# An RWKV block on one core: the planner's cost of a transfer, and a new order for every engine

## The chip, the cores and the metric

The kernel runs on one core of a Trainium2 chip. The core has five engines with a queue of instructions each: TensorE (PE; its weight loads are listed as PEld), VectorE (DVE), ScalarE (ACT), GpSimd (POOL) and SyncE (SP). SP only issues transfers (DMAs); ACT issues some too. An engine works through its own queue in order, and waits at an instruction until what it needs from other engines or from transfers is there. The metric is the time of one execution on the device in microseconds (us), lower is better.

## The reference

One RWKV-6 block over a batch of 8 sequences of 256 tokens and 512 channels, in 32 heads of 16, all in float32. Cut to what matters:

```python
xn = ln(x, ln1); sx = token_shift(xn, state[:, 1])
xxx = tanh((xn + sx * maa_x) @ maa_w1)                  # five groups of 32
x5 = xn + sx * (maa_stack + xxx @ maa_w2)               # k, decay, v, r, g inputs
w = exp(-exp(time_decay + tanh(x5[1] @ decay_w1) @ decay_w2))
r, k, v = x5[3] @ Wr.T, x5[0] @ Wk.T, x5[2] @ Wv.T      # 32 heads of 16
g = silu(x5[4] @ Wg.T)
def step(s, (r, k, v, w)):                              # 256 steps in time
    a = k[:, :, :, None] * v[:, :, None, :]
    return a + w[..., None] * s, einsum(r, u * a + s)
att = group_norm(scan(step)) * gn_w + gn_b
x = x + (att * g) @ Wo.T
xn2 = ln(x, ln2); sx2 = token_shift(xn2, state[:, 0])
rr = sigmoid((xn2 + sx2 * ffn_maa_r) @ ffn_Wr.T)
kk = relu((xn2 + sx2 * ffn_maa_k) @ ffn_Wk.T) ** 2
x = x + rr * (kk @ ffn_Wv.T)
```

## The kernel before, in words

**Work per sequence.** Each of the 8 sequences (b) passes three stages, with channels on the 128 partitions and 256 tokens along the row, mostly as two tiles of 256 channels each (q = 0, 1).

- `inputs_of_scan`: x is loaded (`xt<-in_x`), normed and transposed on TensorE (L503); ACT scales it into `xn` (L509); POOL takes the token shift `sx` (L512); `shifted` makes the first mix (ACT L523, POOL L525); small matmuls (L568, L581, L603) and DVE and POOL (L612, L614) make the five mixed inputs; `project` (L538) multiplies them by the resident weights Wk, Wv, Wr, Wg, and ACT copies or activates the results (L648, L657).
- `scan`: the recurrence runs on VectorE's scan instruction. ACT's queue writes v to DRAM (`vo<-v`, L695). For each of 4 blocks of channels and 4 groups i, SP reads it back as a broadcast over 16 partitions into a tile `vs` (`vs<-vo`, 512 KB, 16 per sequence). ACT sets the first column of it (L711), VectorE multiplies it by k (L714) and scans it into `st` (L716), POOL multiplies `st` by r (L719), and 32 matmuls gather the four groups (L727).
- `rest`: the group norm (ACT L745, PE L753, ACT L758, DVE L760); its scale goes to the partitions that need it in 8 small row copies for each of two tiles (`sq<-sq`, `rk<-sq`, 32 KB, issued by SP) and into `att` (POOL L784, ACT L788), then times g (POOL L790). Then the projection by Wo (`project_tokens`, L553), the second norm and mixes, and the projections by ffn_Wk (L538), ffn_Wr and ffn_Wv (L553) up to the output (DVE L821, POOL L823, `out<-o`). These four weights aren't resident: each is streamed anew for every sequence in two tiles of 512 KB (`Ws<-in_wo`, `Ws<-in_fk`, `Ws<-in_fr`, `Ws<-in_fv`) through a pool of four tiles `Ws`.

All transfers but `vo` are made by the helper `dma` and issued at L359 on SP, in one queue.

**The order of the work.** Nothing is emitted as it is written. Each operation is added to a `Plan` with its engine, an estimated duration, what it writes and reads, and its emitter. There are 2482 of them. The three stages of different sequences are planned to overlap: sequence b's `scan` beside b+1's `inputs_of_scan` and b-1's `rest`. `sequence` gives every operation a rank out of the written table `TURNS` (a permutation of 0 to 2481, in 25 rows: one for the loads at the start, then one for each stage of each sequence). `order` then goes through them as a list scheduler: among the operations whose predecessors have been placed, it takes the lowest rank, puts it off if no buffer of its pool is free, and gives it a start and an end by the durations. The buffer that it takes from a pool is the last one that came free by then. At the end all are sorted by their planned start and emitted, so every engine's queue has the order in which `order` placed them. `TURNS` is the result of a search that is not part of the kernel; the planned end (`span`) is there for it to go by.

**A transfer in the plan.** The engine that issues it (called DMA in the plan) is taken for `us` = 0.6. Then the transfer goes over one `wire`, in turn with all others, at a pace in KB per us, and is there a `lag` after it left the wire. At most eight are in flight: `lanes` holds the landings of the last eight, and an issue waits for the oldest of them. The lag is `LATENCY["DMA"]` (for `vo`, which ACT issues, `LATENCY["ACT"]`) plus what the caller passes: 1.6 for `vs`, 1.2 for `vo`, 0.3 for the row copies.

Of the kernel before, what the change touches and what calls it, by code (L numbers as in the profile page):

```python
# [13 lines left out]
NB, T, E = 8, 256, 512  # L14
# [53 lines left out]
class Plan:  # L68
# [4 lines left out]
    LATENCY = {"PE": 0.3, "DVE": 0.18, "ACT": 0.16, "POOL": 0.12, "DMA": 1.1}  # L73
# [15 lines left out]
    def add(self, engine, us, outs, ins, emit, mode=None, into=(), lag=0.0, kb=0, part=False):  # L89
        outs, ins, into = ([getattr(b, "buf", b) for b in bs] for bs in (outs, ins, into))  # L90
        op = Op(engine, us, outs, ins, emit, mode)
        op.lag, op.wire = self.LATENCY[engine] + lag, kb / 290
# [18 lines left out]
    def stage(self):  # L111
# [6 lines left out]
        316 390 152 382 416 413 475 586 386 300 368 425 948 654 392 44 107 100 185 187 379 151 569 87 545 560 70 602 544  # L118
        66 557 362 54,
        128 192 383 294 166 325 399 223 324 410 351 473 231 254 329 213 338 296 364 175 207 537 19 570 524 371 332 236  # L120
        13 233 232 52 604 287 366 216 712 572 584 556 471 540 615 432 42 45 618 206 677 519 297 527 668 20 428 122 484
        724 398 58 583 673 795 414 241 895 805 75 641 41 607 887 239 752 783 784 261 642 613 47 822 859 694 651 683 855
        357 850 472 397 482 194 523 249 789 897 730 777 791 199,
        215 224 589 276 103 201 278 36 141 619 637 344 120 179 552 253 69 229 157 168 275 794 172 359 568 336 743 920
        251 350 726 839 954 508 707 775 335 643 370 485 751 934 939 219 424 806 346 825 542 129 477 870 1049 1013 901
        240 812 1142 1161 1199 593 975 1063 779 51 1050 178 450 979 421 496 910 448 936 976 1001 749 985 381 848 1002
        952 1172 914 1016 1184 117 610 1123 314 490 1186 722 538 1200 115 412 1217 907 871,
        376 339 452 530 692 408 235 820 461 468 464 669 880 506 470 924 1004 288 658 419 282 1100 995 501 1130 315 438
        1196 930 415 792 719 1211 579 829 807 348 944 330 625 974 1236 462 648 1139 1118 740 852 1084 729 823 925 1232
        1097 274 1210 312 289 427 1209 900 700 1276 867 649 1289 1227 838 1225 188 949 1322 571 1372 796 1292 148 773  # L130
        1195 337 904 1273 1293 1247 1418 1336 1203 1423 318 631 1381 270 354 286 1344 298 682 1466 1096 1467,
        422 1367 1411 1443 95 955 711 174 1262 1468 1456 14 18 457 440 499 163 1334 227 139 234 1491 200 96 1492 843
        1093 1508 1525 1082 1190 1363 1556 653 1112 1171 951 1311 183 781 1037 1044 1582 1083 1590 992 1597 1384 1185
        1310 1622 1429 459 1602 672 420 798 725 541 1117 883 1608 1108 971 1699 1514 844 1631 1688 63 1513 608 474 1640
        1667 1545 817 1397 1007 815 1349 1257 1716 946 238 1765 1669 1309 1755 1653 505 1725 1151 967 1776 1808 189 1802
        1567 1591,
        627 1628 1672 1721 86 1665 1569 1576 1568 1572 1786 577 1204 762 1073 94 293 373 349 539 290 1798 1626 978 1434
        511 1506 1831 1649 1836 40 268 1848 429 387 1401 1126 1129 659 76 1170 1867 903 1166 1313 353 1223 281 634 591
        1470 1393 1924 1436 1791 1538 507 1943 1951 941 1955 28 1882 1368 245 1883 996 1544 1875 59 343 1733 621 378
        1540 1886 588 811 776 614 1392 1661 1908 1921 790 1944 1956 265 1942 1095 1318 1913 363 1280 1998 2019 733 2006  # L140
        1668 2015,
        1079 1069 1070 1074 1072 1577 1714 980 1930 1945 1134 1124 1982 1220 1260 1268 1208 1964 1328 221 244 2012 1999
        1133 1990 1194 1879 1719 2028 1283 91 1287 2050 832 1571 1584 592 1558 1463 1548 1751 638 2044 480 1895 33 272
        1954 1237 1853 1984 1580 2099 340 15 2002 144 2117 1331 754 1644 1675 2076 2086 2129 2068 1596 2027 2107 384
        1421 1424 2065 1465 1624 2043 1893 2009 1231 1358 1937 921 2109 656 1103 2173 2177 818 2119 2146 2154 2126 1647
        10 2207 2110 1587 2196 1634 1809,
        1408 2017 403 2123 623 865 893 1286 1010 186 2150 1102 2157 1224 958 504 1920 2156 1658 1789 1018 1988 1386 1437
        2185 17 1618 1899 2190 834 2194 90 2203 786 1104 1865 1718 1856 727 1554 1619 2253 965 1757 1840 1980 1748 1766
        1962 1143 1154 1121 2267 1305 1793 147 1312 2273 2279 93 2300 761 2212 2105 2104 2216 2238 1923 2237 1315 1712
        1316 885 886 1502 2208 1021 1749 1353 1754 467 2291 1164 1145 130 1430 1756 2281 2270 1314 2101 2290 1376 2244  # L150
        2324 1632 1852 2333 1504 1503,
        1559 2161 2073 1062 133 1060 226 85 195 2274 2264 1605 1858 1614 170 1085 2285 190 196 417 670 2297 1648 628
        2054 322 2318 1623 1555 2323 1887 714 696 766 2328 24 2330 703 664 1179 2158 5 744 2340 1402 2375 2343 2277 2350
        2339 1362 957 1345 2287 380 881 280 2378 2386 1333 2414 1267 702 1738 2387 1694 1404 2363 2345 1600 1997 2360
        1168 1812 2352 2368 826 1727 2379 1565 2251 2400 2374 326 856 2412 2095 2023 1356 2390 2402 2091 2191 479 1850
        2418 299 2427 1635 2460,
        304 389 830 772 447 927 25 30 797 940 29 119 34 543 205 718 375 800 622 431 785 165 915 894 202 667 650 248 495
        735 882 220 911 301 994 258 943 919 559 809 889 701 945 660 456 916 746 458 888 260 666 1017 863 913 65 646 60
        1149 676 851 67 1024 1045 1008 1012 7 8 896 1116 879 518 121 999 1053 446 639 1127 1092 1025 771 307 878 847
        1188 747 1177 1051 699 1167 1019 1022 1132 968 736 39 11 1155 993 1076 585 587 1158 1094 1181 1065 483 1206 50,  # L160
        611 732 739 1099 1009 1265 814 465 1405 113 1255 533 55 88 449 1202 26 1214 502 171 1193 872 127 1242 214 1256
        793 1285 1087 4 1212 497 1284 681 1299 1352 1303 906 1294 16 1351 492 522 1291 478 1323 567 1046 1295 969 1339
        491 828 1234 868 1342 689 1238 1403 1106 821 1330 1327 1395 764 827 1416 763 1320 984 1382 292 1317 1326 1041
        1373 1383 1189 1350 860 1399 1427 68 1432 1481 1370 1355 1445 132 1464 922 1398 1219 1433 1444 1218 1152 1448
        970 1469 1450 1407 1252 1447 1462 273 1499 1509,
        674 1483 566 708 1440 1449 1532 1052 1642 38 1536 198 1417 1486 977 1343 1375 728 1512 720 594 598 1023 1537 156
        1020 1511 1520 1246 43 1187 1412 1517 277 1581 1493 1531 1125 1523 1551 81 1539 1261 1579 361 1611 837 1241 1561
        1270 1615 908 998 1528 1148 1609 966 1541 1645 97 161 1593 1583 1636 1482 1638 1687 102 1321 1620 1663 1709 355
        1213 1550 1630 394 1056 1047 1698 118 1717 1378 1747 655 1656 1705 150 1740 1743 1485 1654 770 1744 1137 961
        1679 803 1745 1026 407 1664 652 1741 1410 250 1800 932,  # L170
        769 1767 780 283 1730 1801 1779 1780 1878 1325 1781 520 1570 1770 986 27 731 697 1670 1677 1773 169 1787 1728
        1290 1505 1557 1790 437 723 902 1005 1794 528 1833 1655 1817 918 813 1564 1832 1281 1813 1198 1742 1838 1821
        1803 1594 1595 1389 164 1680 1804 303 1250 444 1866 372 1400 1039 1854 1824 1822 1841 1239 1872 710 1876 554
        1157 405 1871 1881 1385 1746 1888 1165 1820 1269 564 1898 1221 1914 1939 1910 1900 1859 1915 396 1080 1905 1061
        1925 576 1249 1901 1722 1946 808 1958 1906 1340 1938 933 1068 1258 873,
        748 1947 73 742 217 1989 125 126 1562 1601 1963 341 534 435 553 1949 874 1941 1987 1815 1992 2014 1105 1413 1575
        1979 1388 137 2013 1319 1961 333 1994 1510 2030 1617 1459 1843 2011 2025 1296 134 2022 1678 2040 1245 1527 1604
        2001 2024 1639 876 1111 1976 1173 2039 1861 2070 2082 2079 369 2045 1731 2048 2026 1272 2061 1735 2056 1633 2069
        1533 1932 2053 404 1274 2060 1927 2067 445 846 831 1683 2084 1814 1953 2062 1686 2083 1435 2147 2031 1940 2118
# [73 lines left out]
    def order(self, phases):  # L253
# [7 lines left out]
        while queue:  # L261
# [23 lines left out]
            if op.wire:  # L285
                wire = landed = max(wire, op.end) + op.wire
                lanes.append(landed + op.lag)
# [22 lines left out]
def tile_rwkv_block(  # L310
# [425 lines left out]
    def by_block(t):  # L736
        return t() if len(t().shape) == 3 else t().rearrange("p (m t) -> p m t", m=2)
# [184 lines left out]
```

## Time and profile before

| | |
|---|---|
| median of 3 runs | 703.81 us (702.54 to 704.03) |
| time of the profiled execution | 706.46 us |
| its span, first to last instruction | 704.1 us |
| instructions | 10430 |
| busy: PE, DVE, POOL, ACT | 91%, 80%, 74%, 52% of the span |
| moved by transfers | 127.85 MB, 182 GB/s over the span |
| longest groups | DVE scan L716 289.6 us; POOL L719 254.4 us; DVE L714 152.0 us; PE L553 with mix 117.2 us |
| median time to landing, 512 KB | `vs` 6.9, wo 9.1, fk 6.2, fr 5.7, fv 5.4 us |

How to read the rows that follow: a group is written as line, engine, operation and `out<-in` by the tiles' names, with the number of instructions. `x16` in a row of the timeline is 16 instructions merged. A float32 matmul stands in the trace as two rows of MATMUL, so a call of `project` for half a tile (4 matmuls) is x8. Idle time in brackets is that just before the instruction, with what ended it. A row of waits has who waited, who ended it, the total in us, how often, and the longest. A row of the chain has its start and its length in us. In the rows of slices each digit is a fortieth of the span, in tenths. PEq and SPq are an engine's sequencer.

### The profile page before, as it was taken

To read this page: it belongs to the slowest core of one execution; us is meant where nothing else is said; L and a number is where in the kernel's file an instruction comes from. 1 tells how busy PE (TensorE), PEld (TensorE's weight loads), DVE (VectorE), ACT (ScalarE), POOL (GpSimd) and SP (SyncE) were. 2 spreads that over 40 slices of the span, in tenths; PEclk is the share of its full clock that TensorE was granted. 3 is DMA by queue.
4 is the path that set the end of the run, shared out by engine and by line. 5 is a ranking of instruction groups with operands and counts; after the bars stand their busy time and mean duration, and the time that the engine had idled before them with its cause. 6 is when DMAs were issued, how large, how long until landed. Compare 5 with 4: busy or idle time off the path is not lost.

```text
span 704.1 us, 10430 instructions
## 1 busy us (share of the span) xinstructions
PE 638.5 (91%) x3752; PEld 427.2 (61%) x3752; DVE 565.3 (80%) x567; ACT 366.2 (52%) x757; POOL 520.3 (74%) x426
## 2 busy tenths in 40 slices
PE   4999999898998999799999998998996997598987
PEld 4786877656465864567745864766564674445453
DVE  1679999999998999877999779998988678685300
ACT  4644544358733774338753656547644357346250
POOL 3759986899897897957798775888968478567141
PEclk9999999999999999899999999999998999699999
DMA  9598583759778872938695794859648197764432
GB/s 295 197 260 240 151 197 90 175 140 241 193 197 222 192 216 74 260 101 202 173 277 145 224 239 126 215 149 267 159 114 201 39 255 193 186 180 143 134 112 89
DMA packets 57603, 127.85 MB, mean 182 GB/s; under 512 B 7568, under 2 KB 16272, under 8 KB 57552
## 3 DMA queue, kind: packets, MB, share of 16 engines
q1 hardware_dynamic: 53200, 123.00, 66.1%
q10 hardware_dynamic: 4352, 4.20, 1.8%
q8 instruction: 29, 0.48, 0.3%
q14 instruction: 22, 0.18, 0.1%
HBM read 115.11 MB, written 8.39 MB: 175 GB/s over the span
## 4 chain that ended last, share of the span: by engine, by line
PE 36%; DMA 25%; DVE 16%; POOL 8%; issue 6%; ACT 5%; SPq 3%; POOLq 0%; DVEq 0%; ACTq 0%
PE ps L553 15%; DMA vs<-vo 14%; PE ps L538 12%; DVE st L716 8%; DVE vs L714 4%; DMA Ws<-in_fk 4%; SPq L359 3%; DMA Ws<-in_wo 3%; PE ps L603 3%; PE ps L727 3%; POOL st L719 3%; POOL mix L525 2%; DVE mix L612 2%; DMA vo<-v 1%; POOL sx L512 1%
## 5 line engine op out<-in xcount | busy, mean ns | idle before, releaser
L716 DVE TENSOR_TENSOR_SCAN st<-wrep,vs 128x1024 f32<-128x1024 f32 x128 | 289.6, 2282 | 8.6 <-ACT wrep L701 4.5
L719 POOL TENSOR_TENSOR st<-st,r 128x1024 f32<-128x1024 f32 x128 | 254.4, 1999 | 54.8 <-DVE st L716 43.5
L714 DVE TENSOR_TENSOR vs<-vs,ps 128x1024 f32<-128x1024 f32 x128 | 152.0, 1211 | 29.2 <-ACT vs L711 28.4
L553 PE MATMUL ps<-Ws,mix 128*128 128x512 f32 x256 | 117.2, 600 | 4.1 <-DVE vs L714 2.2
L614 POOL TENSOR_TENSOR mix<-mix,xn 128x512 f32<-128x512 f32 x80 | 85.5, 1090 | 17.7 <-DVE mix L612 17.7
L553 PEld LDWEIGHTS ps<-Ws,mix 128*128 128x128 f32 x256 | 46.9, 190 | 59.6 <-issue 49.3
L538 PE MATMUL ps<-mix,Ws 128*128 128x256 f32 x256 | 62.4, 403 | 16.1 <-DMA Ws<-in_fk 7.8
L711 ACT ACTIVATE vs<-s,cm 128x4 f32<-128x4 f32 x128 | 35.5, 295 | 79.6 <-DMA vs<-vo 74.8
L553 PE MATMUL ps<-Ws,g 128*128 128x512 f32 x128 | 62.5, 643 | 12.3 <-DMA Ws<-in_wo 6.8
L612 DVE SCALAR_TENSOR_TENSOR mix<-ps,vec,sx 128x256 f32<-128x256 f32 x160 | 65.4, 478 | 9.4 <-PE ps L603 9.3
L538 PEld LDWEIGHTS ps<-mix,Ws 128*128 128x128 f32 x256 | 51.3, 203 | 26.3 <-DMA Ws<-in_fk 8.2
L727 PE MATMUL ps<-st,con 128*32 128x256 f32 x1024 | 62.3, 382 | 1.5 <-ACT mix L805 1.2
L525 POOL TENSOR_TENSOR mix<-mix,xn 128x512 f32<-128x512 f32 x48 | 51.6, 1090 | 13.0 <-ACT mix L523 12.8
L538 PE MATMUL ps<-mix,Wg 128*128 128x256 f32 x256 | 59.2, 384 | 1.8 <-DMA Wg<-in_wg 1.1
L538 PE MATMUL ps<-mix,Wr 128*128 128x256 f32 x256 | 58.3, 382 | 2.4 <-POOL mix L614 2.3
L538 PE MATMUL ps<-mix,Wv 128*128 128x256 f32 x256 | 58.9, 383 | 0.0
L538 PE MATMUL ps<-mix,Wk 128*128 128x256 f32 x256 | 58.2, 383 | 0.0
L538 PEld LDWEIGHTS ps<-mix,Wg 128*128 128x128 f32 x256 | 47.7, 190 | 12.6 <-issue 3.3
L538 PEld LDWEIGHTS ps<-mix,Wr 128*128 128x128 f32 x256 | 48.0, 190 | 10.6 <-POOL mix L614 2.7
L538 PEld LDWEIGHTS ps<-mix,Wv 128*128 128x128 f32 x256 | 47.9, 190 | 10.4 <-issue 4.3
L538 PEld LDWEIGHTS ps<-mix,Wk 128*128 128x128 f32 x256 | 48.0, 190 | 9.8 <-issue 2.7
L553 PEld LDWEIGHTS ps<-Ws,g 128*128 128x128 f32 x128 | 25.7, 206 | 45.4 <-issue 28.6
(85 smaller groups left out, 826.7 us busy)
## 6 DMA issues: line engine op xcount, KB each, us to landing
vs<-vo SPq DMA_DIRECT2D x128, 512.0 KB, 6.9
Ws<-in_wo SPq DMA_DIRECT2D x16, 512.0 KB, 9.1
Ws<-in_fk SPq DMA_DIRECT2D x16, 512.0 KB, 6.2
Ws<-in_fr SPq DMA_DIRECT2D x16, 512.0 KB, 5.7
Ws<-in_fv SPq DMA_DIRECT2D x16, 512.0 KB, 5.4
xt<-in_x SPq DMA_DIRECT2D x8, 512.0 KB, 7.0
x<-in_x SPq DMA_DIRECT2D x8, 512.0 KB, 5.2
vo<-v ACTq DMA_DIRECT2D x16, 256.0 KB, 2.2
```

What stands on the lines that cost most here:

```text
L359: plan.add("DMA", 0.6, [out] if out else [], [src] if src else [], lambda: nc.sync.dma_start(out=dst(), in_=in_()), lag=lag, kb=kb, part=part)
L525: gp(512, t, [t, xn[q]], lambda q=q, t=t: nc.gpsimd.tensor_tensor(t(), t(), xn[q]()[:, :, 1 : T + 1], ALU.add))
L538: nc.tensor.matmul(ps()[:, m, :], lhsT=w[k]()[:, o : o + P], rhs=src[k // 2]()[:, k % 2, :], start=(k == 0), stop=(k == NK - 1),)
L553: nc.tensor.matmul(ps().rearrange("p m t -> p (m t)"), lhsT=src[h]()[:, k % 2, n * P : (n + 1) * P], rhs=w[k](), start=(k == 0), stop=(k = ...
L603: nc.tensor.matmul(ps[g, q]()[:, m, :], lhsT=w2()[lo : lo + MAA, k * P : (k + 1) * P], rhs=ta()[lo : lo + MAA, i, :], start=True, stop=True,)
L612: dve(256, [t], [p_, vec, sx[q]], lambda g=g, q=q, m=m, t=t, p_=p_: nc.vector.scalar_tensor_tensor(t()[:, m, :], p_()[:, m, :], col(f"maa_ ...
L614: gp(512, t, [t, xn[q]], lambda q=q, t=t: nc.gpsimd.tensor_tensor(t(), t(), xn[q]()[:, :, 1 : T + 1], ALU.add))
L711: act(4, vs, [s0, cm], lambda i=i, blk=blk, vs=vs: nc.scalar.activation(vs()[:, :, 0:1], s0()[:, blk, 4 * i : 4 * i + 4].rearrange("p (n o ...
L714: dve(4 * T, [vs], [vs, kp], lambda m=m, vs=vs, kp=kp: nc.vector.tensor_tensor(vs(), vs(), kp()[:, m : m + 1, :].to_broadcast([P, 4, T]), ...
L716: dve(4 * T, [st], [w, vs], lambda w=w, vs=vs, st=st: nc.vector.tensor_tensor_scan(st().rearrange("p n t -> p (n t)"), w().rearrange("p n ...
L719: gp(4 * T, st, [st, r], lambda m=m, st=st, r=r: nc.gpsimd.tensor_tensor(st(), st(), r()[:, m : m + 1, :].to_broadcast([P, 4, T]), ALU.mult))
L727: nc.tensor.matmul(pat()[32 * i : 32 * i + 32, 0, :], lhsT=con()[:, s : s + 32], rhs=done[i]()[:, j, :], start=(j == 0), stop=(j == 3),)
```

## The change

Five edits in the plan's description of a transfer, and a new table of ranks. The operations, their emitters, tiles and pools are the same.

- The transfer takes the wire from 1.2 us behind its start (or when the wire is free), in place of from the end of its issue, 0.6 behind its start.
- The wire's pace is 245 KB per us in place of 290.
- The lag common to all is 0.8 in place of 1.1; beyond it, `vs` gets 0.8 in place of 1.6, `vo` 0.0 in place of 1.2, the row copies 0.0 in place of 0.3.
- All 25 rows of `TURNS` are new.

```diff
-    LATENCY = {"PE": 0.3, "DVE": 0.18, "ACT": 0.16, "POOL": 0.12, "DMA": 1.1}
+    LATENCY = {"PE": 0.3, "DVE": 0.18, "ACT": 0.16, "POOL": 0.12, "DMA": 0.8}
...
-        op.lag, op.wire = self.LATENCY[engine] + lag, kb / 290
+        op.lag, op.wire = self.LATENCY[engine] + lag, kb / 245
...
     TURNS = """
-        316 390 152 382 416 413 475 586 386 300 368 425 948 654 392 44 107 100 185 187 379 151 569 87 545 560 70 602 544
-        66 557 362 54,
...
+        389 659 273 446 513 525 531 621 752 397 431 577 766 828 794 350 679 580 374 359 441 560 170 210 628 546 540 180
+        612 129 607 212 489,
...
     """
...
             if op.wire:
-                wire = landed = max(wire, op.end) + op.wire
+                wire = landed = max(wire, op.start + 1.2) + op.wire
                 lanes.append(landed + op.lag)
...
                 plan.add("ACT", 0.37, [vo], [v], lambda v=v, vo=vo: nc.scalar.dma_start(
-                    out=vo().rearrange("m p t -> p m t"), in_=v()[:, :, 0:T]), lag=1.2, kb=262)
+                    out=vo().rearrange("m p t -> p m t"), in_=v()[:, :, 0:T]), lag=0.0, kb=262)
...
                 dma(vs, lambda i=i, m=m, vo=vo: vo()[m, 32 * i : 32 * i + 32].rearrange("(h j) t -> h (j t)", j=4).unsqueeze(0)
-                    .to_broadcast([S, HB, 4 * T]), lambda vs=vs: vs().rearrange("p j t -> p (j t)"), 524, vo, 1.6)
+                    .to_broadcast([S, HB, 4 * T]), lambda vs=vs: vs().rearrange("p j t -> p (j t)"), 524, vo, 0.8)
...
                         dma(rsb, lambda blk=2 * q + n: rs()[32 * blk : 32 * blk + 32, 0:T],
-                            lambda n=n, rows=rows, rsb=rsb: by_block(rsb)[rows, n, :], 32, rs, 0.3, True)
+                            lambda n=n, rows=rows, rsb=rsb: by_block(rsb)[rows, n, :], 32, rs, 0.0, True)
```

## The prediction

> **What bounds the kernel now.** I read the page first (its busy shares and its slices), then windows of 84 us (about one batch each), then the waits of TensorE, then the chain and the timeline at TensorE's long waits, then single transfers. The page's busy line and three rows of its slices:
>
> ```profile
> PE 638.5 (91%) x3752; PEld 427.2 (61%) x3752; DVE 565.3 (80%) x567; ACT 366.2 (52%) x757; POOL 520.3 (74%) x426
> PE   4999999898998999799999998998996997598987
> PEclk9999999999999999899999999999998999699999
> DMA  9598583759778872938695794859648197764432
> ```
>
> TensorE (PE) is the bound. It works 638.5 us of the 704.1 us span, so 65.6 us are idle, and no order of the same work ends much before 651: 638.5, the 7.11 us wait for the first weights, and 5.5 us behind the last matmul (698.6 to 704.1). What an order can win is part of the rest, some 53 us. The windows say where it lies (columns: busy time of each engine, granted clock, DMA share, GB/s):
>
> ```profile
> 30.00:114.00 84.00, 81.69 (x574) 63.75 (x576) 75.70 (x78) 40.70 (x89) 65.93 (x50) 1.00 0.76 195
> 114.00:198.00 84.00, 76.70 (x497) 50.90 (x491) 83.16 (x78) 49.91 (x104) 74.07 (x57) 1.00 0.67 169
> 450.00:534.00 84.00, 81.83 (x511) 55.81 (x511) 77.87 (x75) 47.92 (x100) 68.53 (x53) 1.00 0.72 186
> 534.00:618.00 84.00, 65.57 (x367) 43.08 (x365) 61.05 (x46) 41.04 (x79) 57.61 (x42) 0.88 0.68 167
> ```
>
> The six windows from 30 to 534 have TensorE busy 81.69, 76.70, 80.36, 78.16, 81.15 and 81.83 us, a mean of 79.98. The window 534 to 618 has 65.57 and a clock of 0.88: one stretch holds 18.4 us of the idle time. Who ended TensorE's waits:
>
> ```profile
> PE ps L538 <- DMA Ws<-in_fk: 7.8, 1, 7.8
> PE ps L462 <- DMA Ws<-in_wv: 7.1, 1, 7.1
> PE ps L553 <- DMA Ws<-in_wo: 6.8, 2, 6.0
> PE ps L538 <- POOL mix L525: 5.4, 2, 3.2
> PE ps L553 <- POOL att L689: 4.0, 1, 4.0
> ```
>
> Apart from the first load (wv), the two largest are weights that landed late, and both are in that stretch. The chain through it:
>
> ```profile
> 529.20 13.79 DMA Ws<-in_wo
> 543.13 9.46 PE ps L553 x16
> ...
> 569.64 15.49 DMA Ws<-in_fk
> ...
> 588.99 6.21 DMA vs<-vo
> ...
> 595.26 11.29 DMA Ws<-in_fk
> 606.60 9.34 PE ps L538 x28
> ```
>
> A weight tile of 512 KB took 11 to 15 us from issue to landing there. The same kind of transfer with the queue empty (first line: issued at 225.0), and one of the broadcasts that feed the scan, also alone (issued at 79.8), with the microseconds to landing last:
>
> ```profile
> Ws<-in_fk SPq DMA_DIRECT2D x1, 512.0 KB, 3.3
> vs<-vo SPq DMA_DIRECT2D x1, 512.0 KB, 4.4
> ```
>
> So lateness is queueing, and the plan's order of issues decides it. The last thing to see is the price of a long wait beyond the wait itself; four merged rows of TensorE's timeline:
>
> ```profile
> 375.04 7.11 PE L553 MATMUL ps<-Ws,g 128*128 128x512 f32 x16 [0.83 <-DMA Ws<-in_wo]
> 543.13 9.46 PE L553 MATMUL ps<-Ws,g 128*128 128x512 f32 x16 [5.97 <-DMA Ws<-in_wo]
> 606.60 9.32 PE L538 MATMUL ps<-mix,Ws 128*128 128x256 f32 x28 [7.82 <-DMA Ws<-in_fk]
> 638.24 7.17 PE L538 MATMUL ps<-mix,Ws 128*128 128x256 f32 x32 [2.13 <-POOL mix L525]
> ```
>
> The same 16 matmuls take 2.35 us more after a wait of 5.97 than after 0.83. The 28 after 7.82 take 9.32, where 28/32 of 7.17 is 6.27: 3.05 more. The granted clock is 0.83 in 530 to 550 and 0.73 in 590 to 610.
>
> **The change, part by part.** No instruction is added or removed; every engine, SP's and ACT's queues included, gets another order.
>
> *The constants.* Alone they move nearly nothing. The planner takes the ready operation of lowest rank whatever the clock says, so they touch which free buffer is taken and the merge of engines, not the order on an engine: cost 0, covered by the ranks being what sorts. What they tell is how good a guide the search had. A 512 KB weight load alone lands by the old formula after 0.6+1.81+1.1 = 3.51 us, by the new after 1.2+2.14+0.8 = 4.14 (trace 3.3). A broadcast: 5.11 and 4.94 (trace 4.4). The copy of v to DRAM: 2.63 and 2.43 (median in the trace 2.2). A small row copy: 2.11 and 2.13 (medians 1.9 and 2.6). So alone, neither is better. In a queue they part: each further 512 KB costs the old plan 1.81 us, the new 2.14. In the trace nine transfers of 512 KB queued from 281.5 on landed between 286.69 and 303.52, which is 16.83/8 = 2.10 us apart; five broadcasts issued from 397.1 to 399.9 landed 2.4 apart. I laid both formulas over the issue times of all transfers of this trace. The old one has the wo loads land 2.57 us too early on average, fk 1.69, fr 1.17, the broadcasts 0.87; the new one 0.33 early, 0.02 early, 0.30 late and 0.01 late. For the 90 transfers that took over 8 us: 2.48 early by the old, 0.39 early by the new. The new one is worse at the start, where the resident weights land 2.5 to 4 us before it says. So the old search could believe that the weights at 543 and 606 would be there, and the new one could not.
>
> The Trainium skill, page "DMA: Bandwidth & Descriptors", section "Anatomy of one DMA — SWDGE (gpsimd) path", speaks against this: fitted there for another issuing path, about 2.0 us fixed plus bytes over 436 GB/s, so that 290 is too slow already and 245 further off. By it a load alone takes an estimated 3.2 us, as here, but the next would follow 1.2 us behind; the rows above show 2.10. By the page the change gains nothing; the trace decides for the change.
>
> *The ranks.* All but 13 of the 2482 ranks differ, by 352 places in the median. What moves past what can't be enumerated, so I bound the outcome by rows. What late transfers cost TensorE now: 5.97+2.35 (wo at 543), 7.82+3.05 (fk at 606), 0.83 (wo at 375), and two waits for the product of a late broadcast, 2.81 at 597.65 and 1.93 at 429.90: 24.8 us. That is the upper end of the gain. The lower end is 0 or a loss: the queue carries the same 123 MB, a weight load put ahead of four broadcasts (as wo at 529.20, behind those of 526.13 to 528.09) lands 4 x 2.1 = 8.4 us sooner and makes them 2.1 later, and then VectorE's scan is late next (in this trace ACT already waits 74.8 us for broadcasts in 42 places). What I take is from the nearest row, the other windows: bring 534 to 618 up to the worst of the six (76.70) and 11.1 us return, up to their mean and 14.4 do. Half of the 24.8 is 12.4, between these two. The tail behind 618 has too little work left to fill its waits, and I leave it as it is; the start (the wait of 7.11, 1.64 and 1.15 more to 57 us) too, between 3 us won and 3 lost, since what is issued first there is bound by the pace.
>
> The clock is a second place for a rule. The skill's page "TensorE: Matmul & The Clock Gate", Part 1, has the clock halve after an idle window of about 3.4 us and stay so for about as long: an estimated 1.7 us lost per long wait, against 2.35 and 3.05 in the rows. By the page the upper end is 22.8 in place of 24.8, and half of it 11.4.
>
> *Sum.* The profiled execution took 706.46 us (span 704.1 and 2.4 around it), 2.65 above the median of 703.81. 706.46 - 12.4 = 694.1; less 2.65 it is 691.4 on the scale of the median, 1.8% faster.
>
> **The rivals.**
>
> *All late transfers go, or other idle time with them.* For it: in four of the six windows TensorE is idle under 4 us. Against it: the windows at the end hold fewer batches to choose from. 703.8 - 24.8 = 679.
>
> *The gain is handed back.* One stall goes and others of its size come, because a rank moved by hundreds of places is a new draw for the POOL and DVE waits too (5.4 on mix, 4.0 on att), which the old and the new constants cost alike. For it: TensorE's wait of 4.0 us at 296 has no late transfer behind it. About 704, 699 to 709.
>
> *Slower, by a clump in the SP queue.* From 569.64 to 585.15 SP mostly stood for transfers in flight to land before it could issue the next; 16 small row copies came behind six broadcasts and three weight tiles, and POOL waited 6.61 us for them at 604. If the new order puts such a clump before a projection in one of the full batches, and leaves the stall at 606 or one like it in place, it costs what that one costs, 7.82+3.05 = 10.9: 714.7. It decides from the point where such clumps cost more than the stalls that went. For it: the plan overstates a lone weight load (4.14 against 3.3) and the start, so loads are drawn early and together. Against it: the new formula sees exactly these queues.
>
> *The change doesn't do what it says*, that is, a better formula is no better order: this is the second rival's number, 704.
>
> **How the numbers follow.** Half recovered (683 to 699): 0.40. All or more (672 to 683): 0.12. Handed back (699 to 709): 0.18, cut evenly into faster, same and slower. Slower (709 to 724): 0.30. Faster 0.40+0.12+0.06 = 0.58; same, within 0.2% (1.4 us either way, about what a measurement of this kernel can tell), 0.06; slower 0.36. The time is the likeliest case's, 691.4, its own range 683 to 699. The range 677 to 718 leaves out about half of the second case (0.06) and the end of the slower one (0.12).
>
> **What would show it.** Right: no wait of TensorE above 3 us ended by a weight load after the first 60 us; the fullest late window at 76 us busy or more and no window of 84 us with a clock under 0.95; the weight loads' median time to landing down from 9.1 (wo) toward 6; the bytes and instruction counts as before, give or take table loads. Wrong: new rows of "PE <- DVE vs" or "PE <- POOL" that sum to more than what left the DMA rows; SP standing again for landings in a full batch; a longer wait than 7.1 us before the first matmul; or the end of the scan (last broadcast now issued at 626.6) later than now, since what follows it, 77 us, has little to lie beside.

## The result and the profile after

The changed kernel takes 672.44 us in the median (671.73 to 674.6) beside 703.92 for the kernel before: a ratio of 0.9552, 95% interval 0.9513 to 0.9591. That is 31.5 us faster. The forecast was 691.4 with a range of 677 to 718, so the direction was right and the time lies 4.6 us below the range. The rival "all late transfers go, or other idle time with them" (679) came nearest. Medians in this document are of fast executions: one of 1662 us (the constants alone) and one of 1310 us (the load moved by hand) are left out.

The page after, the same rows as before (busy times, then slices of 16.8 us):

```profile
PE 635.9 (95%) x3752; PEld 427.5 (64%) x3752; DVE 563.2 (84%) x567; ACT 369.0 (55%) x761; POOL 520.1 (77%) x426
PE   3999999989899999999999999999999999798987
PEclk9799999979999999999999999999999999899989
DMA  9479848387769886687888488857885588935422
```

The engines do the same work in less time: TensorE was busy 638.5 us and is busy 635.9, its idle time went from 65.6 to 36.9. The two sum to 2.6 + 28.7 = 31.3 us, which is the difference of the spans (704.1 and 672.8). The windows of the kernel after (busy time of each engine, clock, DMA share, GB/s):

```profile
114.00:198.00 84.00, 77.87 (x477) 52.86 (x476) 80.42 (x77) 51.94 (x108) 69.38 (x54) 0.96 0.72 181
282.00:366.00 84.00, 84.00 (x500) 56.86 (x502) 79.84 (x80) 51.04 (x105) 75.89 (x60) 1.00 0.82 221
450.00:534.00 84.00, 83.25 (x485) 55.52 (x484) 78.85 (x77) 48.09 (x96) 70.29 (x53) 1.00 0.70 185
534.00:618.00 84.00, 75.71 (x459) 48.63 (x457) 71.14 (x56) 50.59 (x100) 66.15 (x50) 0.96 0.70 183
```

Two windows in the middle have TensorE busy without a gap (282 to 366 and 366 to 450, 84.00 us of 84), and the stretch 534 to 618 went from 65.57 to 75.71. (The same stretch of time does not hold the same work in both kernels, since the changed one is ahead by then.) TensorE's longest waits after:

```profile
PE ps L463 <- DMA Ws<-in_consts: 7.1, 1, 7.1
PE ps L539 <- POOL mix L526: 5.6, 3, 3.2
PE ps L582 <- POOL mix L526: 3.6, 2, 3.3
PE ps L539 <- ACT v L649: 3.0, 1, 3.0
PE ps L504 <- ACT xh L492: 2.7, 3, 1.5
```

Behind the first load (the same 7.1 as before) no row names a transfer any more. Three of the four streamed weights and the broadcasts land sooner in the median, though the same bytes move in 4% less time: wo 6.9 us (9.1 before), fk 5.6 (6.2), fr 4.9 (5.7), the broadcasts 6.5 (6.9). One lands later, fv, with 6.5 (5.4). ScalarE's waits for broadcasts fell from 74.8 us in 42 places to 47.4 in 26 (the kernel before first):

```profile
ACT vs L711 <- DMA vs<-vo: 74.8, 42, 6.4
ACT vs L712 <- DMA vs<-vo: 47.4, 26, 8.8
```

By stretch, from the windows of both kernels, TensorE's idle time in us is:

| stretch | before | after | less by |
|---|---|---|---|
| 0 to 30 | 10.4 | 11.9 | -1.5 |
| 30 to 534 | 24.1 | 8.6 | 15.5 |
| 534 to the end | 31.0 | 16.4 | 14.6 |

So the late stretch gave 14.6 us, about what the prediction had for it. The middle, for which it had nothing, gave 15.5.

### The profile page after: what moved, and what is told of

It is laid out like the page before. It is cut to its first block, busy times and chain, and to the rows that moved or that the text cites. A ratio compares the mean times of both kernels' runs of the same rounds, so it can differ in the third digit from the quotient of the medians.

```text
span 672.8 us, 10449 instructions
## 1 busy us (share of the span) xinstructions
PE 635.9 (95%) x3752; PEld 427.5 (64%) x3752; DVE 563.2 (84%) x567; ACT 369.0 (55%) x761; POOL 520.1 (77%) x426
## 2 busy tenths in 40 slices
DMA packets 57603, 127.85 MB, mean 190 GB/s; under 512 B 7568, under 2 KB 16272, under 8 KB 57552
## 4 chain that ended last, share of the span: by engine, by line
PE 65%; DVE 16%; DMA 7%; POOL 4%; issue 4%; ACT 2%; SPq 0%; POOLq 0%; DVEq 0%; ACTq 0%
PE ps L539 29%; PE ps L554 19%; DVE st L717 8%; PE ps L728 6%; DMA vs<-vo 5%; DVE vs L715 4%; PE ps L604 3%; DVE mix L613 2%; PE ps L582 2%; PE ps L569 2%; PE ps L504 2%; POOL st L720 1%; POOL mix L526 1%; POOL sx L513 1%; DMA sq<-sq 1%
## 5 line engine op out<-in xcount | busy, mean ns | idle before, releaser
L720 POOL TENSOR_TENSOR st<-st,r 128x1024 f32<-128x1024 f32 x128 | 254.4, 2000 | 33.8 <-DVE st L717 27.9
L728 PE MATMUL ps<-st,con 128*32 128x256 f32 x1024 | 63.8, 385 | 3.5 <-ACT mix L806 1.4
L539 PE MATMUL ps<-mix,Wr 128*128 128x256 f32 x256 | 61.8, 396 | 3.1 <-ACT v L649 3.0
L539 PE MATMUL ps<-mix,Ws 128*128 128x256 f32 x256 | 59.4, 389 | 5.6 <-POOL mix L526 5.6
L712 ACT ACTIVATE vs<-s,cm 128x4 f32<-128x4 f32 x128 | 34.6, 294 | 48.1 <-DMA vs<-vo 47.4
L554 PE MATMUL ps<-Ws,g 128*128 128x512 f32 x128 | 59.3, 615 | 0.7 <-POOL g L791 0.6
L539 PEld LDWEIGHTS ps<-mix,Ws 128*128 128x128 f32 x256 | 49.1, 194 | 16.1 <-POOL mix L526 8.1
L539 PEld LDWEIGHTS ps<-mix,Wr 128*128 128x128 f32 x256 | 49.9, 198 | 12.3 <-ACT v L649 3.4
L728 PEld LDWEIGHTS ps<-st,con 128*32 128x32 f32 x1024 | 31.0, 110 | 30.7 <-issue 7.4
```

The costliest lines, as they stand in the source:

```text
L539: nc.tensor.matmul(ps()[:, m, :], lhsT=w[k]()[:, o : o + P], rhs=src[k // 2]()[:, k % 2, :], start=(k == 0), stop=(k == NK - 1),)
L554: nc.tensor.matmul(ps().rearrange("p m t -> p (m t)"), lhsT=src[h]()[:, k % 2, n * P : (n + 1) * P], rhs=w[k](), start=(k == 0), stop=(k = ...
L712: act(4, vs, [s0, cm], lambda i=i, blk=blk, vs=vs: nc.scalar.activation(vs()[:, :, 0:1], s0()[:, blk, 4 * i : 4 * i + 4].rearrange("p (n o ...
L720: gp(4 * T, st, [st, r], lambda m=m, st=st, r=r: nc.gpsimd.tensor_tensor(st(), st(), r()[:, m : m + 1, :].to_broadcast([P, 4, T]), ALU.mult))
L728: nc.tensor.matmul(pat()[32 * i : 32 * i + 32, 0, :], lhsT=con()[:, s : s + 32], rhs=done[i]()[:, j, :], start=(j == 0), stop=(j == 3),)
```

## The experiments

**The constants alone, and the ranks alone.** Theory: the ranks carry everything and the constants only guided the search that made them. The first kernel has the new constants with the old table, the second the old constants with the new table.

```diff
-    LATENCY = {"PE": 0.3, "DVE": 0.18, "ACT": 0.16, "POOL": 0.12, "DMA": 1.1}
+    LATENCY = {"PE": 0.3, "DVE": 0.18, "ACT": 0.16, "POOL": 0.12, "DMA": 0.8}
...
-        op.lag, op.wire = self.LATENCY[engine] + lag, kb / 290
+        op.lag, op.wire = self.LATENCY[engine] + lag, kb / 245
```

> The new constants of a transfer with the old table of ranks. Every engine's order stays the kernel before's to the last operation; 343 of 1256 buffers lie in another tile of their pool. Theory A (the ranks carry the whole change, the constants only guided the search): within 0.5% of before, 700 to 707 us. Rival B (the choice of the free tile by truer landings takes away waits for tiles): 1 to 2% faster, 690 to 697 us. Rival C (tiles chosen by another clock than the order was searched with collide): 710 us or more.

Measured: 707.36 us beside 704.18, ratio 1.0037 (1.0006 to 1.0067).

```diff
     TURNS = """
-        316 390 152 382 416 413 475 586 386 300 368 425 948 654 392 44 107 100 185 187 379 151 569 87 545 560 70 602 544
-        66 557 362 54,
...
+        389 659 273 446 513 525 531 621 752 397 431 577 766 828 794 350 679 580 374 359 441 560 170 210 628 546 540 180
+        612 129 607 212 489,
...
```

> The old constants of a transfer with the new table of ranks. Every engine's order is the changed kernel's; 364 of 1256 buffers lie in another tile. Theory A: 672 us as the changed kernel, within 4 us. Rival B (the constants help through the tiles): 680 us or more.

Measured: 675.47 us, ratio 0.9609 (0.9539 to 0.9679), where the changed kernel has 0.9552. Theory A holds: the constants change no engine's order, only which free tile is taken. That made the old order 0.37% slower and the new one some 0.6% faster, the second within what its intervals leave open.

**One late load moved by hand.** The wo tile on which TensorE waited 5.97 us at 543 is issued ahead of the broadcasts it stood behind. Its rank goes from 2364 to 2331, just ahead of the broadcast issued at 521.7; the 33 ranks between move up by one, and the order on TensorE, ScalarE and GpSimd stays. VectorE's order does not: since the planner places what is ready by rank, the sum `x` behind the projection by Wo (L796) comes ahead of seven operations of the scan (five L714, two L716) that stood before it.

```diff
     TURNS = """
...
-        2351 688 2171 1936 2364 2335 2286 645 105 854 2078 1676 2381 532 1479 679 640 1259 252 225 1535 1689 2131 1692
...
+        2352 688 2171 1936 2331 2336 2286 645 105 854 2078 1676 2381 532 1479 679 640 1259 252 225 1535 1689 2131 1692
...
```

> The kernel before, with one load moved: the wo tile that was issued at 529.20, behind four broadcasts, gets a rank that puts it ahead of them, so that it is issued at about 522. Theory of the prediction (a late weight load costs its wait and the slow clock behind it): TensorE's wait of 5.97 us at 543 goes, with 2.35 us of slow clock, 8.3 us in all: 695.5 us. Half of it, 4 us, if the broadcasts that now come 2.1 us later are felt: 699.5 us. Rival (the stall is handed on whole to the next late transfer, since fk at 606 has the last word in that stretch): no change, 702 to 705 us.

Measured: 703.24 us, ratio 0.999 (0.9955 to 1.0025). Nothing is won, as the rival had it, but the run doesn't say why, because it moved more than the load. In the kernel before, VectorE worked on those seven ahead of TensorE's wait for wo and in it, and stood still only behind them, 6.22 us at `x`; the seven ended with the three merged in the first of these rows:

```profile
539.52 3.46 DVE L714 TENSOR_TENSOR vs<-vs,ps 128x1024 f32<-128x1024 f32 x3
549.20 0.69 DVE L796 TENSOR_TENSOR x<-ps,x 128x512 f32<-128x512 f32 x1 [6.22 <-PE ps L553]
```

With the load moved they come behind that product. The planner of the changed kernel would have told: by the new constants the kernel before is planned to end at 703.7 us and this order at 703.4. In that plan TensorE's wait of 3.3 us at the projection by Wo goes, and one of 4.8 us comes ahead of the next sequence's decay projection, for a mix that GpSimd makes behind that scan's products. Whether the chip lost the time there, or at fk, or because the second wo tile, now third in line, waited for its buffer and held SP, stays open.

**Only the transfers reordered.** This kernel has the changed kernel's constants, and the old ranks for everything but the transfers. Theirs were moved by a short search of mine, by the planned end under the new constants.

```diff
     TURNS = """
-        316 390 152 382 416 413 475 586 386 300 368 425 948 654 392 44 107 100 185 187 379 151 569 87 545 560 70 602 544
-        66 557 362 54,
...
+        62 96 43 86 82 516 576 65 713 72 644 521 998 541 483 165 226 219 35 33 76 268 647 206 624 637 191 674 623 188
+        633 461 176,
...
```

(All numbers differ since the ranks are counted anew; the order among the other operations is that of the old table.)

> The changed kernel's constants, the ranks of the kernel before except those of the transfers, which a short search moved under the new constants (the plan's own end goes from 703.7 to 672.5). TensorE's order is the kernel before's to the last operation; 288 of the 361 places in SP's queue hold another transfer, and 63 places on VectorE, 155 on ScalarE and 27 on GpSimd differ, through what waited for a buffer. Theory A (before lost its time to transfers that came in the wrong order, and TensorE's waits on GpSimd and ScalarE in the middle were late transfers too): 676 to 686 us, with TensorE's idle time from 30 to 534 us under 15 us. Rival B (the new order of the compute engines carries the gain): 695 us or more. By the prediction's sum, which gave the transfers 12.4 us: 691.

Measured: 684.03 us, ratio 0.9699 (0.965 to 0.9747): 20 us of the 31.5 with TensorE's order untouched (some places on the other three engines changed, as said above). From 30 to 534 us TensorE is idle 504 - 488.86 = 15.1 us, where it was 24.1 before and the expectation said under 15:

```profile
30.00:534.00 504.00, 488.86 (x3004) 334.55 (x3002) 468.83 (x459) 281.37 (x587) 420.03 (x327) 0.99 0.74 193
```

Before, the same stretch of the trace was:

```profile
30.00:534.00 504.00, 479.89 (x2979) 329.12 (x2980) 459.98 (x453) 276.86 (x579) 411.34 (x322) 0.99 0.72 187
```

And the wait of 4.00 us that the trace before put down to GpSimd at 296 is gone; that of 2.76 at 214 is still there with 2.21. Over the whole span of 680.3 us TensorE is idle 43.7 us:

```profile
PE 636.6 (94%) x3752; PEld 427.1 (63%) x3752; DVE 564.7 (83%) x567; ACT 365.1 (54%) x757; POOL 520.8 (77%) x426
```

Against the 65.6 of before that is 21.9 less: 0.7 in the first 30 us, 9.0 in the middle and 12.2 behind 534. The rest of the changed kernel's gain, 10 to 12 us of time, 6.5 us of idle time in the middle among it, comes only with the new orders of the computing engines. Fewer waits for broadcasts are not what they bring: ScalarE waits 50.2 us for them here and 47.4 in the changed kernel.

**The search blinded again.** The old constants, and a search that goes on from the new ranks by the old constants alone. It takes 1.9 us off the planned end.

```diff
     TURNS = """
-        389 659 273 446 513 525 531 621 752 397 431 577 766 828 794 350 679 580 374 359 441 560 170 210 628 546 540 180
-        612 129 607 212 489,
...
+        269 1153 83 1032 1096 928 1081 1060 1039 645 304 1162 1102 1172 53 584 650 155 42 71 751 921 26 280 909 935
+        152 368 966 387 1040 878 297,
...
```

> The old constants, and ranks searched on from the changed kernel's by the old constants alone. Their plan ends at 658.5, which is 9.6 us sooner than the plan of the kernel before (668.1) and, by the same old constants, 1.9 us sooner than the changed kernel's ranks (660.4). By the new constants the same ranks end at 687. Theory A (the gain is the search's seeing late transfers, and goes again when it doesn't): 687 to 700 us. Rival B (the new ranks are simply the longer search, whatever a transfer costs): 668 to 674 us.

Measured: 692.99 us, ratio 0.9828 (0.9778 to 0.9878). Better by its own plan, this order is 20 us slower than the one it started from. Some of TensorE's waits for streamed weights are back:

```profile
PE ps L555 <- DMA Ws<-in_fv: 5.6, 2, 3.9
PE ps L540 <- DMA Ws<-in_fk: 3.7, 1, 3.7
PE ps L555 <- DMA Ws<-in_wo: 1.4, 1, 1.4
```

So the changed kernel's gain is not just a longer search: a search carried further without sight of the queue loses most of it (of 31.5 us, 11.2 are left).

**Smaller loads in both kernels.** Order and tiles stay; only the queue gets lighter. In 60 of the 64 loads of streamed weights a quarter of the tile is brought, the rest keeps old values, so that the products are not the reference's.

```diff
+    def stream_load(h, t, src):
+        if id(t.place) in full:
+            nc.sync.dma_start(out=t()[:, 0, 0 : E // 2], in_=src[2 * h * P : (2 * h + 1) * P, 0 : E // 2])
+        else:
+            full.add(id(t.place))
+            nc.sync.dma_start(out=t(), in_=src[2 * h * P : (2 * h + 2) * P, :].rearrange("(k p) e -> p k e", p=P))
...
-        load_pairs(tiles, src)
+        for h, t in enumerate(tiles):
+            plan.add("DMA", 0.6, [t], [], lambda h=h, t=t: stream_load(h, t, src), kb=524)
```

> The kernel before, but of the streamed weights (wo, fk, fr, fv) 60 of 64 loads bring only a quarter of their tile, 131 KB in place of 524 KB; the rest of the tile keeps what it held, so the products are not the reference's. Every engine's order and every buffer are the kernel before's. Theory A (late transfers cost before what the change won): about 680 us, 676 to 686, with TensorE's waits of 4.0 us on GpSimd at 296 and of 2.8 on ScalarE at 214 gone, too. Rival B (its order of compute is poor): 695 us or more.

Measured: 684.43 us, ratio 0.9702 (0.9652 to 0.9751). All engines' orders are those of before here, and it is as fast as the run with the transfers reordered. So 20 us can be had without any change of order on the computing engines. In the middle TensorE is idle 13.9 us, where it was 24.1:

```profile
30.00:534.00 504.00, 490.15 (x3010) 335.37 (x3010) 470.49 (x460) 281.53 (x589) 421.35 (x329) 0.99 0.64 161
```

> The changed kernel with the same cut loads as the run before it, order and buffers as in the changed kernel; the products are not the reference's. Theory A: nothing waits for a transfer there any more, so 668 to 673 us. Rival B (fewer bytes make any order faster, by contention): 660 us or less.

Measured: 667.88 us, ratio 0.9479 (0.9425 to 0.9534). The same relief is worth 3.0% to the order of before (20 us) and at most 0.7% to the new one (ratios of 0.9552 and 0.9479, 5 us), where the intervals overlap and the changed kernel's later runs, 0.9518 and 0.9514, leave 0.4%. What remains between the two with light loads, 684.4 - 667.9 = 16.5 us, is hardly the weights' lateness (the lightened kernel before has one wait of TensorE for a streamed weight, 1.0 us): the order of the other work, or the broadcasts, which are as large as ever. Which of the two, this pair doesn't show: ScalarE's waits for broadcasts are 48.2 us in the one and 33.8 in the other. Of TensorE's middle waits in the kernel before, 4.00 at 296 and 2.76 at 214 don't appear in the lightened one (0.21 is left at the second), as expected; 2.33 on a mix of GpSimd at 133 stays (2.39).

**A better order.** If the loss that remains is lateness too, an order that still works when transfers are later than counted should be faster. The ranks were searched on from the changed kernel's by the mean of three plans, with transfers as counted, slower and quicker.

```diff
     TURNS = """
-        389 659 273 446 513 525 531 621 752 397 431 577 766 828 794 350 679 580 374 359 441 560 170 210 628 546 540 180
-        612 129 607 212 489,
...
+        499 1153 241 839 994 1079 1171 933 1238 752 726 1205 1296 1278 347 1095 1108 257 432 295 817 1008 178 9 1015
+        767 524 440 1036 227 1056 628 245,
...
```

> The changed kernel's constants, and ranks searched on from its own by the mean of three plans: the transfers as the changed kernel counts them, 8% slower and 0.6 us later, and 11% quicker and 0.2 us sooner. Its plan by the new constants ends at 660.4, 1.2 us later than the changed kernel's 659.2; the mean of the three is 662.3 against 672.7. Theory A, carried on (what is lost between the plan's 659 and the measured 672 are transfers that come later than the plan says, in an order that fits the plan too closely): 664 to 670 us. Rival (what is lost there has nothing to do with transfers): 672 to 677 us.

> The changed kernel as it is, beside the run before it on the same chip: 672 to 676 us by every theory.

Measured: 665.17 us (ratio 0.9443, 0.9384 to 0.9503) beside 670.58 for the changed kernel (0.9518, 0.9456 to 0.9581), which is 1.4 us under what was expected of it. The intervals against before overlap, so both were run again:

> The robust order again, in more rounds: 665 us, 0.5 to 1.3% under the changed kernel of the same chip, if the difference of the two runs before is real; the same as it within 0.3% if it was noise.

> The changed kernel beside the robust order, on the same chip in as many rounds: 669 to 674 us by every theory.

Measured: 665.0 us (0.9457, 0.9417 to 0.9496) beside 669.22 (0.9514, 0.9475 to 0.9554). The intervals overlap slightly again, but in both comparisons the difference has the same sign and size, 5.4 and 4.2 us: over ten runs each the robust order took 662.7 to 667.6, the changed kernel 665.0 to 673.9. It is the fastest of all kernels here that give the reference's result, by some 0.7%. That it is faster because late transfers hurt it less is what it was searched for. The traces agree: ScalarE's waits for broadcasts are about half of the changed kernel's on the same chip, 19.9 against 46.5 us in the first comparison,

```profile
ACT vs L713 <- DMA vs<-vo: 19.9, 16, 3.7
ACT vs L712 <- DMA vs<-vo: 46.5, 27, 6.5
```

and 23.5 against 42.0 in the second. That these waits and not the other changes of order make the difference is not shown.

**The plan's end against the chip.** Every order here has a planned end by each set of constants, reckoned after the result was known:

| ranks | by the old constants | by the new | measured |
|---|---|---|---|
| before | 668.1 | 703.7 | 704 |
| before, one load moved | 676.3 | 703.4 | 703 |
| transfers reordered | 670.6 | 672.5 | 684 |
| searched on by the old constants | 658.5 | 687.0 | 693 |
| the changed kernel's | 660.4 | 659.2 | 672 |
| robust | 661.3 | 660.4 | 665 |

The old constants put the order that measured 693 first. The new ones rank all but the last two as the chip does (the first two rows are too close to rank), and the two orders on which no search went by them they hit within 1 us. That searched on by the old constants, which began from one searched by the new, comes out 6 us later than planned, the two that were searched by the new alone 11 to 13 us. That a search also finds what the plan gets wrong in its favour would explain it; it is argued, not shown. The robust order is 5 us later than planned. So the new plan promised 44.5 us from before to the changed kernel (703.7 to 659.2), and 31.5 came.

## Why the prediction was wrong, point by point

- **"The constants alone move nearly nothing": right.** 0.37% slower with the constants alone; no operation changes its place on an engine.
- **The new formula fits the transfers: right, and on the new trace too.** (For the 90 slow transfers of before the issue times give 0.1 to 0.2 us early, where the prediction has 0.39, and the resident weights at the start land 1.4 to 5.7 us before the formula says, where it has 2.5 to 4; the reading stays.) Laid over the issue times of the kernel after, the old formula is 0.75 us early on average over all transfers and 2.16 us for the 62 that took over 8 us; the new one is 0.15 late and 0.22 early. That the plan under the new constants reproduces the time of the old order within 1 us agrees with it, though that is the order on whose trace the fit was seen.
- **The Trainium skill's page "DMA: Bandwidth & Descriptors", section "Anatomy of one DMA — SWDGE (gpsimd) path",** has 2.0 us fixed, then bytes over 436 GB/s, fitted for another issuing path. By the prediction's reading of it there would have been no gain. The trace of after keeps the pace seen before (ten transfers of 512 KB queued from 284.0 on landed 2.02 us apart, where the nine from 281.5 on landed 2.10 apart before), and the order made by the slower, later counting won 4.5%. Here the measurement decides against applying that figure to a queue of such transfers.
- **"What late transfers cost TensorE now: 24.8 us" as the upper end: wrong.** The gain of 31.5 lies above it, and the sum was short of late transfers besides. It took the waits that the trace puts down to a transfer or to the product of a late broadcast, and left out those that it puts down to another engine. Two of those were late transfers. At 296 the timeline of TensorE and GpSimd in the kernel before has:

```profile
296.32 4.61 PE L553 MATMUL ps<-Ws,g 128*128 128x512 f32 x5 [4.00 <-POOL att L689]
295.10 1.09 POOL L689 TENSOR_TENSOR att<-v,att 128x512 f32<-128x512 f32 x1
```

  and the transfer of the wo tile that was issued at 283.93 (microseconds to landing last):

```profile
Ws<-in_wo SPq DMA_DIRECT2D x1, 512.0 KB, 12.3
```

  The matmul reads Ws and g, and `att` of that GpSimd operation is no input of it. The operation ended at 296.19, the wo tile landed at 283.93 + 12.25 = 296.18, and the matmul began at 296.32. The two fell into 0.01 us, and the row names the one that isn't needed. The wait is gone with the transfers reordered and with small loads. The rival "handed back" even used this wait as an example of one with no late transfer behind it. At 214 the way is longer (timeline of ScalarE and TensorE, before):

```profile
212.83 0.30 ACT L711 ACTIVATE vs<-s,cm 128x4 f32<-128x4 f32 x1 [2.45 <-DMA vs<-vo]
213.16 1.17 ACT L683 COPY att<-ps 64x512 f32<-64x512 f32 x2
214.38 1.13 PE L633 MATMUL ps<-w,dw 64*128 64x256 f32 x8 [2.76 <-ACT att L683]
```

  ScalarE stood 2.45 us at the broadcast's first column, the copy behind it in its queue came late for that, and TensorE waited for the copy. With small loads this wait goes too. 4.00 with the slow clock behind it (16 matmuls in 9.99 us, against 7.11: 2.88) and 2.76 make 9.6 us more, so that the upper end by the same reckoning was at least 34.4. As a price that is too high: taking most of the lateness away in two ways, by order and by lighter weight loads, gave 20 us each time. What carried the gain past 24.8 was, as far as these runs tell, the other engines' new order.
- **"Half of the 24.8 is 12.4", with the six other windows left as they are and nothing for the other engines' new order: the step that failed.** For the late stretch the 12.4 was near (14.6, of which 12.2 with the transfers alone); but half was a choice between two rows, so that is in part luck. The windows' mean of 79.98 busy was taken as what an order can reach. It was itself lowered, and the middle gave 15.5 us of idle time in place of none: 9.0 with the transfers reordered, 6.5 only with the computing engines' new orders. In time, the transfers were worth 20 us in place of 12.4, and the other engines' order 10 to 12 in place of nothing. Which of those new orders did it stays open.
- **Pricing stall by stall: not settled for one load, rather too high in total.** The single moved load won nothing of the 8.3 us priced for it, but VectorE's order changed with it. All transfers moved together won 20, where the prediction counted 24.8 and a fuller count gives 34.4.
- **What would show it: mostly right.** wo's median went from 9.1 toward 6 (6.9), the late window reached 75.71 us busy of the 76 asked for, no full window has a clock under 0.96, and the bytes are the same. The last broadcast is issued at 596.6 (626.6 before).
- **The rival "slower, by a clump in the SP queue": did not come.** After the first load no wait of TensorE is put down to a weight at all. Its example was also read too simply: of the 15.5 us from 569.64 to 585.15, SP's longest wait, 6.6 us, was for VectorE's result `sq` (L760), which the row copies carry; 6.2 us were waits for landings. The rival of the first load to be worse didn't either: 7.12 for 7.11; the first 30 us are 1.5 us poorer.
- **The clock.** After the waits of 3.26 at 15.2 and 3.23 at 645.4 in the kernel after, the matmuls lose 1.79 (3.78 against 1.99 for the same eight before) and 1.69 (32 in 8.86, against 7.17). Before, after 4.00, 5.97 and 7.82, it was 2.88, 2.35 and 3.05. The Trainium skill's page "TensorE: Matmul & The Clock Gate", Part 1, would charge an estimated 1.7 us to a long wait (half of the 3.4 us for which it has the clock halved). That fits the waits of a little over 3 us, and is short for the longer ones.

## What to carry to other kernels

Where an order comes out of a planner, check the planner's costs against the trace's issue and landing times before costing the new order, and ask what the same plan says of the old order under the corrected costs: here it said 703.7 where 704 was measured and 668.1 had been planned, and so how much of the loss the plan had not seen. The same question, put to the order with one load moved, would have said that it wins nothing. A wait that a profile puts down to another engine can be a late transfer at one remove, or one that landed in the same instant; look at what the waiting instruction reads, and at what the named engine had itself waited for. Stalls are not a sum: windows that look good can suffer from the same cause as the bad one, and stalls priced at 24.8 us, or 34.4 with those overlooked, were worth 20 when the transfers moved. And an experiment on one instruction in a planned kernel has to be checked on every engine's queue, since the planner may move others with it.

## What the runs showed of the hardware that was not expected

Under load, transfers of 512 KB on one queue landed some 2.1 us apart (2.02 to 2.40 in the bursts named above), and the lateness of a burst reached engines that read none of it: ScalarE held by a broadcast for 2.45 us made TensorE wait 2.76. No byte had to go to get rid of TensorE's waits for it: the same 127.85 MB at 190 GB/s (182 before) leave TensorE without a wait for a streamed weight, when they are issued in another order.
